# Selective scans: projection by token halves, the other direction added at another turn, part of B's diagonals on ScalarE

## The chip, the cores and the metric

The kernel runs on one core of a Trainium2 chip. The engines used here are TensorE (PE in the profile, with its weight loads as PEld), VectorE (DVE), ScalarE (ACT), GpSimd (POOL) and the queue of SyncE (SP), which issues the DMAs. Each works through its own list of instructions in order, and waits on semaphores for the others. The metric is the device time of one execution in microseconds.

## The reference, cut to what matters

The network has two layers; the change touches the scans in the second one's mixer. For each of K = 4 directions, with D = 256 channels, N = 16 states, R = 8 ranks and L = 4096 tokens in each of B = 4 images:

```python
x_dbl = jnp.einsum('bkdl,kcd->bkcl', xs, x_proj_w)
dts_r, Bs, Cs = (x_dbl[:, :, :R], x_dbl[:, :, R:R + N], x_dbl[:, :, R + N:])
dts = jnp.einsum('bkrl,kdr->bkdl', dts_r, dt_proj_w)
dt = jax.nn.softplus(dts + dt_proj_b[None, :, :, None])
A = -jnp.exp(A_logs).reshape(K, d, N)
def step(h, inp):
    dt_l, u_l, B_l, C_l = inp
    dA = jnp.exp(dt_l[..., None] * A)
    h = h * dA + (dt_l * u_l)[..., None] * B_l[:, :, None, :]
    y = jnp.einsum('bkdn,bkn->bkd', h, C_l)
    return (h, y)
ys = ys + Ds.reshape(1, K, d, 1) * xs
y = ys[:, 0] + ys[:, 2][..., ::-1]
y1 = ys[:, 1] + ys[:, 3][..., ::-1]
```

Directions 2 and 3 run backwards through the tokens, 0 and 1 forwards; 0 and 2 go by rows of the image, 1 and 3 by columns.

## The kernel before, in words

Attention, a recurrent layer, the inputs of the scans, the scans, their outputs and the experts follow one another. All that is told here lies in the function `scans`.

The tokens of the four images, padded to 4125 each, are cut into blocks of 125, and four blocks make a window of W = 500 tokens: 33 windows a direction, 132 in all, in the order of directions 2, 3, 0, 1. A window has 16 tiles: four groups of four states (q), by four blocks. One tile holds, for 128 channels on the partitions, both halves of the channels (h), four states and one block, 1016 elements wide with the places for the carried values.

The order of the work is written out by hand: the loop at the end runs over turns p, and every instruction stands where the turn puts it. In turn p the following are issued, in this order: `finish` of a window whose turn it is; the `fill` of tile p + 1; the `carry` of tile p − 1; the scan of tile p; two sums; `times_c` of tile p; the load of C for tile p + 5; the load of the other direction; the decays; and steps of `project` for the windows ahead. A window's tiles start at its turn 0, and 16 turns later the next one's do. So turns are counted modulo 16 here: a step that `project` yields as −14 is in turn 2 of the window before its own.

What a tile needs:

- `fill` (line 1291): TensorE makes dt·u·B for the tile. The weights are dt·u turned so that tokens are on the partitions (`dtu_t`), the moving operand is a diagonal matrix of B's values (`b_diag`, and `b_other` with the halves of the partitions exchanged), 32 x 128 at a time. Between them TensorE adds zeros to y (line 1300).
- decays (line 1256): ScalarE's exponentials, into a ring of 12 tiles, three or two in each of most turns; none in turns 2, 3, 10 and 11.
- scan (line 1315): one VectorE instruction over the tile.
- `carry` (line 1336): ScalarE copies the last state of tile p − 1 into the ring of decays, for the next tile of the same states. That tile is two turns on, so the carry has one scan's time to be done without a wait.
- `times_c` (line 1349): GpSimd multiplies the states by C, which DMAs have spread over the partitions (`c_ring`, from `c_rows` in device memory).
- sums (line 1366): TensorE adds the products into y, in even turns, 16 records at a time. The last sum of a window is in turn 8 of the next.

What a window needs is in `project`, a generator whose steps are spread over 40 turns: load u; x_ps = w_x·u (line 1144, one 500-column product per half of the channels, turns 15 and 1); copy it to `xd` on ScalarE (line 1149, turn 2), with a row of ones; send C's rows to device memory (line 1151); copy B's rows in pieces of 32 tokens (`b_rows`, line 1158, turn 3); the dt projection (line 1163, turn 9); softplus by exponentials and logarithms on ScalarE (lines 1182 to 1190, turns 10 to 12) and a maximum on VectorE, which writes dt (line 1195, turns 13 and 14); dt·u on GpSimd (line 1198, turn 15); turn B's rows (line 1203, turn 1); make `b_diag` (turns 2 and 3); copy dt·u in pieces (`quarters`, line 1227); exchange halves by two DMAs (line 1232, turn 4); turn dt·u (line 1239, turn 5) and copy it (line 1241, turn 6). x_ps, the dt projections, B's turned rows and dt·u's all use one PSUM tile `mm` of two banks. `b_diag` is made as a product of B's values with an identity of 32 columns, `ident32`: VectorE does two of the four groups of partitions' tokens in turn 2 (line 1213, 1024 elements) and one in turn 3 (512 elements); GpSimd does the fourth from a copy (`b_sb`, line 1206).

At the end of a window, `add_other` (line 1377) adds to y, on TensorE, either D·u (direction 2) or the result of the opposite direction (0 and 1); for direction 3 it returns at once. It stands in turn 23 of the window, turn 7 of the next. What it adds is loaded in turn 13. `finish` (line 1387) copies y to `sum` on ScalarE in turn 25, turn 9 of the next, the first instruction of that turn, and stores it.

Of the kernel before, what the change touches and what calls it, by code (L numbers as in the profile page):

```python
# [19 lines left out]
F32 = mybir.dt.float32  # L20
AF = mybir.ActivationFunctionType
# [5 lines left out]
P = 128  # L27
# [7 lines left out]
D, N, R, K = 256, 16, 8, 4  # L35
ND = D // P
NB, BLOCK = 4, 125
DT_ROWS = 0, 96
LP = -(-L // BLOCK) * BLOCK
E, HID, TOPK = 64, 512, 8  # L40
NHC = HID // P
# [957 lines left out]
def scans(ctx, tc, a, us, ys, flag):  # L999
# [10 lines left out]
    nc = tc.nc  # L1010
    cst = ctx.enter_context(tc.tile_pool(name="sc_c", bufs=1))
# [5 lines left out]
    NW = B * JB // NB  # L1017
    assert NW * NB == B * JB
    TILES = Q * NB
    HALF = P // 2  # L1020
    S = T + 2
    LANE = 4 * S

    RINGS = 12, 4, 12
    C_RING = 8
    SKIP = CH - LANE

    ident = cst.tile([P, P], F32, name="ident")
# [8 lines left out]
        rows = slice(HALF * i, HALF * i + HALF)  # L1037
        nc.vector.tensor_copy(fold[rows], ident[rows, rows])
    w_x = loaded(nc, cst, a["w_x"], "w_x")
    w_dt = cst.tile([P, K, P], F32, name="w_dt")  # L1040

    one = cst.tile([P, 1], F32, name="one")
    nc.vector.reduce_sum(one, ident[:, R : R + 1 + DT_ROWS[1] : DT_ROWS[1]], axis=AX.X)
    for h, row in enumerate(DT_ROWS):
        nc.sync.dma_start(w_dt[row : row + R + 1], a["w_dt"][:, :, h * P : (h + 1) * P])
    ds = loaded(nc, cst, a["ds"], "ds")
    na = loaded(nc, cst, a["a_logs"], "a_logs")
    nc.scalar.activation(na, na, AF.Exp)
# [72 lines left out]
    def quartered(of, to, turned):  # L1121

        for half in range(2) if turned else (None,):
            i = NB if half is None else NB // 2
            yield (
                to if half is None else to[:, :, 2 * half : 2 * half + 2],
                bass.AP(
                    of.tensor,
                    of.offset + (0 if half is None else (2 - 2 * half) * T),
                    [of.ap[0], [STEP, NS], [T, i], [1, 32]],  # L1130
                ),
            )

    def project(v):

        k = v.k
        yield -BEFORE
        v.u = work.tile([P, ND, W], F32, tag="u", name="u")
        for b, of, to in v.pieces:
            nc.sync.dma_start(v.u[:, :, to], us[b][k % 2][:, :, of])  # L1140
        x_ps = mm[:, 0]
        for h, turn in enumerate((-33, -31)):
            yield turn
            nc.tensor.matmul(
                x_ps[:, :W], w_x[:, h, k, :], v.u[:, h, :], start=h == 0, stop=h == ND - 1
            )
        yield -30
        xd = work.tile([P, W], F32, tag="xd", name="xd", bufs=1)
        nc.scalar.activation(xd, x_ps[:, :W], AF.Identity, bias=one)
        v.c_rows = dram.tile([NB, N, T], F32, tag="c", name="c_rows")  # L1150
        nc.sync.dma_start(
            v.c_rows.rearrange("i n t -> n i t"),
            xd[64 : 64 + N].rearrange("n (i t) -> n i t", i=NB),
        )
        yield -29
        b_rows = work.tile([32 + N, NS, NB, 32], F32, tag="b_rows", name="b_rows", bufs=1)
        for to, of in quartered(xd[32 : 32 + N], b_rows[32:], False):
            nc.scalar.copy(to, of)
        yield -23
        pts = mm[:, :, :W]  # L1160
        for h, row in enumerate(DT_ROWS):
            rows = slice(row, row + R + 1)
            nc.tensor.matmul(pts[:, h], w_dt[rows, k, :], xd[rows], start=True, stop=True)
        yield -22
        e = work.tile([P, ND, W], F32, tag="e", name="e", bufs=1)
        if v is todo[0]:

            nc.scalar.preload_act_table_set("natural_log_exp_and_others")
        low = work.tile([P, ND * NS * P], F32, tag="low", name="low", bufs=1)
        bound = low[:, : ND * W].rearrange("p (h t) -> p h t", h=ND)  # L1170
        if flag is None:
            nc.scalar.activation(e, pts, AF.Relu, scale=-1.0, bias=most)
            nc.scalar.activation(e, e, AF.Exp, scale=-1.0, bias=most)
            nc.scalar.activation(bound, e, AF.Copy, scale=-0.5, bias=1.0)
            yield -21
            nc.gpsimd.tensor_mul(bound, bound, e)
            for h in range(ND):
                nc.vector.tensor_max(bound[:, h], pts[:, h], bound[:, h])
            nc.scalar.activation(pts, e, AF.Ln, bias=1.0)
        else:  # L1180
            nth = todo.index(v)
            nc.scalar.activation(
                bound, pts, AF.Exp, scale=-1.0, accum_out=largest[:, 1, nth : nth + 1]
            )
            nc.scalar.activation(e, pts, AF.Exp, accum_out=largest[:, 0, nth : nth + 1])
            yield -21
            nc.scalar.activation(bound, bound, AF.Ln, bias=half)
            nc.scalar.activation(pts, e, AF.Ln, bias=1.0)
            yield -20
            nc.scalar.activation(bound, bound, AF.Exp, scale=-1.0)  # L1190
        yield -19
        v.dt = work.tile([P, ND, W], F32, tag="dt", name="dt")
        for h, turn in enumerate((-19, -18)):
            yield turn
            nc.vector.tensor_max(v.dt[:, h], pts[:, h], bound[:, h])
        yield -17
        dtu = work.tile([P, ND, W], F32, tag="e", name="dtu", bufs=1)
        nc.gpsimd.tensor_mul(dtu, v.dt, v.u)
        yield -15
        b_ps = mm[:, 1, : NS * N].rearrange("p (s n) -> p s n", s=NS)  # L1200
        for i in range(NS):
            part = b_rows[32 : 32 + N, i].rearrange("n i t -> n (i t)")
            nc.tensor.transpose(b_ps[:, i, :], part, ident[32 : 32 + N, 32 : 32 + N])
        yield -14
        b_sb = work.tile([P, N], F32, tag="b_sb", name="b_sb")
        nc.scalar.copy(b_sb, b_ps[:, NS - 1, :])
        v.b_diag = work.tile([P, NS, N, 32], F32, tag="b_diag", name="b_diag")
        quarters = work.tile([P, ND, NS, NB, 32], F32, tag="low", name="quarters", bufs=1)
        for turn, i in ((-14, 0), (-13, 2)):
            yield turn  # L1210
            h = i // 2
            w = 2 - h
            nc.vector.tensor_mul(
                v.b_diag[:, i : i + w].rearrange("p s n t -> p (s n) t"),
                b_ps[:, i : i + w]
                .rearrange("p s (n o) -> p (s n) o", o=1)
                .to_broadcast([P, w * N, 32]),
                ident32.rearrange("p (o t) -> p o t", o=1).to_broadcast([P, w * N, 32]),
            )
            if h:  # L1220
                nc.gpsimd.tensor_mul(
                    v.b_diag[:, NS - 1],
                    b_sb.rearrange("p (n o) -> p n o", o=1).to_broadcast([P, N, 32]),
                    ident32.rearrange("p (o t) -> p o t", o=1).to_broadcast([P, N, 32]),
                )
            for to, of in quartered(dtu[:, h], quarters[:, h], h):
                nc.scalar.copy(to, of)
# [12 lines left out]
        yield -10  # L1240
        nc.scalar.copy(v.dtu, turned)
# [164 lines left out]
    with tc.manual_schedule():  # L1406
# [58 lines left out]
        def sums(p):  # L1465

            g, turn = divmod(p - 10, NB)
            for g, n in ((g, 0), (g, 1)) if turn == 0 else ((g, 2), (g, 3)) if turn == 2 else ():
                if g in range(len(pairs)):
                    sum_of(pairs[g], n)  # L1470
            w, turn = divmod(p - 23, TILES)
            if turn == 0 and w in range(len(todo)):
                add_other(todo[w])

# [317 lines left out]
def laid_out(i):  # L1792
# [15 lines left out]

    def apart(w):

        out = np.zeros((K, P, D), w.dtype)
        out[:, 32 : 32 + N], out[:, 64 : 64 + N] = w[:, R : R + N], w[:, R + N :]
        for row in DT_ROWS:
            out[:, row : row + R] = w[:, :R]
        return out

    def turned(w):
# [23 lines left out]
        "w_x": apart(i["L1_conv_x_proj_w"]).reshape(K, P, ND, P).transpose(3, 2, 0, 1),  # L1841
# [36 lines left out]
```

## Time and profile before

| | us |
|---|---|
| time, median of 3 executions (lowest to highest) | 9429.01 (9418.11 to 9439.51) |
| the profiled execution: time, span | 9417.97, 9416.2 |
| first scan begins, last scan ends | 3582.72, 8748.46 |
| PE, DVE, ACT, POOL busy in the span | 8705.1, 8349.7, 7121.8, 4993.6 |
| in 4900 to 6140 (direction 3): PE, DVE, ACT, POOL | 1181.2, 1224.9, 1068.6, 1192.9 of 1240 |
| in 6180 to 7420 (direction 0): PE, DVE, ACT, POOL | 1184.5, 1205.3, 1047.2, 1165.7 of 1240 |
| one scan, of 2112 | 2.256 |
| one product with C on GpSimd, of 2112 | 2.152 |
| one decay on ScalarE, of 4224 | 0.715 |

In the scans all four engines are nearly always busy, and PE's busy time includes pipelined ends. So sums of busy time decide little there: it is the order inside of a window, the same 132 times, that shows who waits. The groups of instructions give durations, the timeline of each engine gives starts, and a bracket behind a line of the timeline gives the idle time before it and what ended it.

### The profile page before, as it was taken

To read this page: it belongs to the slowest core of one execution; us is meant where nothing else is said; L and a number is where in the kernel's file an instruction comes from. 1 tells how busy PE (TensorE), PEld (TensorE's weight loads), DVE (VectorE), ACT (ScalarE), POOL (GpSimd) and SP (SyncE) were. 2 spreads that over 40 slices of the span, in tenths; PEclk is the share of its full clock that TensorE was granted. 3 is DMA by queue.
4 is the path that set the end of the run, shared out by engine and by line. 5 is a ranking of instruction groups with operands and counts; after the bars stand their busy time and mean duration, and the time that the engine had idled before them with its cause. 6 is when DMAs were issued, how large, how long until landed. Compare 5 with 4: busy or idle time off the path is not lost. (4 is left out here: it accounts for less than half of the span.)

```text
span 9416.2 us, 237919 instructions
## 1 busy us (share of the span) xinstructions
PE 8705.1 (92%) x102194; PEld 4318.3 (46%) x102194; DVE 8349.7 (89%) x5102; ACT 7121.8 (76%) x10926; POOL 4993.6 (53%) x2433
## 2 busy tenths in 40 slices
PE   7999999999988888999999999999999999999766
PEld 3333333333323334555555555555555555555223
DVE  6999999999978318999999999999999999999764
ACT  3888888888856467888888888888888888888321
POOL 0000000000001017999999999999999999999100
PEclk8999999999999898999999999999999999999887
DMA  4000000000011335666666656666666666666634
GB/s 169 36 8 35 8 10 35 8 8 8 10 52 56 115 135 151 173 173 173 172 171 167 165 164 162 161 171 173 173 173 173 173 173 173 173 173 168 231 111 184
DMA packets 530963, 1164.77 MB, mean 124 GB/s; under 512 B 76818, under 2 KB 444506, under 8 KB 502106
## 3 DMA queue, kind: packets, MB, share of 16 engines
q1 hardware_dynamic: 529882, 1149.30, 42.0%
q8 instruction: 807, 13.22, 0.6%
q14 instruction: 274, 2.24, 0.1%
HBM read 828.51 MB, written 182.15 MB: 107 GB/s over the span
## 5 line engine op out<-in xcount | busy, mean ns | idle before, releaser
L1315 DVE TENSOR_TENSOR_SCAN states<-decays,db 128x1016 f32<-128x1016 f32 x2112 | 4671.3, 2256 | 109.1 <-ACT decays L1336 60.5
L1349 POOL TENSOR_TENSOR products<-states,c_ring 128x1000 f32<-128x1000 f32 x2112 | 4459.8, 2152 | 294.8 <-DVE states L1315 173.4
L1256 ACT ACTIVATE decays<-dt,a_logs 128x500 f32<-128x500 f32 x4224 | 3018.2, 715 | 86.6 <-DVE states L1315 0.5
L1291 PEld LDWEIGHTS db<-b_diag,dtu_t 32*128 32x128 f32 x16896 | 2051.1, 187 | 1523.1 <-DVE states L1315 927.4
L1291 PE MATMUL db<-b_diag,dtu_t 32*128 32x128 f32 x16896 | 2429.4, 283 | 245.1 <-DVE states L1315 226.2
L1291 PE MATMUL db<-b_other,dtu_t 32*128 32x128 f32 x16896 | 2454.2, 284 | 0.0
L1300 PE MATMUL y<-zeros 32*128 32x128 f32 x14720 | 2122.0, 283 | 0.0
L1291 PEld LDWEIGHTS db<-b_other,dtu_t 32*128 32x128 f32 x16896 | 2048.0, 186 | 0.3 <-issue 0.2
L1366 PE MATMUL y<-products,ident 64*64 64x500 f32 x16896 | 2018.8, 592 | 1.1 <-POOL products L1349 1.1
L1300 PEld LDWEIGHTS y<-zeros 32*128 32x128 f32 x14720 | 1771.9, 186 | 0.0
L342 DVE TENSOR_TENSOR total<-total,ring 128x2048 f32<-128x2048 f32 x768 | 1706.9, 2285 | 32.3 <-ACT ring L304 31.6
masks.py:197 POOL MEMSET ident<- 128x128 f32 x6 | 1.2, 206 | 2915.6 <-SPq L181 2622.9
L304 ACT ACTIVATE ring<-sa 128x2048 f32<-128x2048 f32 (+3 forms) x667 | 1153.7, 1738 | 273.8 <-PE sa L289 262.2
L314 PE MATMUL av<-ring,v_at 128*32 128x256 f32 (+1 forms) x16128 | 1096.1, 389 | 6.2 <-ACT o L323 5.7
L1366 PEld LDWEIGHTS y<-products,ident 64*64 64x64 f32 x16896 | 541.2, 132 | 696.7 <-issue 568.1
L314 PEld LDWEIGHTS av<-ring,v_at 128*32 128x32 f32 x16128 | 421.4, 109 | 950.9 <-issue 748.9
L304 ACT ACTIVATE ring<-sb 128x1536 f32<-128x1536 f32 (+2 forms) x585 | 800.6, 1375 | 73.6 <-PE sb L289 63.8
L289 PE MATMUL sa<-q_at,k_at 32*128 32x512 f32 x4898 | 701.4, 640 | 20.6 <-issue 14.3
L289 PE MATMUL sb<-q_at,k_at 32*128 32x512 f32 x3294 | 624.0, 641 | 0.0
L1336 ACT COPY decays<-states 128x8 f32<-128x8 f32 x2048 | 405.3, 198 | 212.2 <-DVE states L1315 196.0
L289 PEld LDWEIGHTS sa<-q_at,k_at 32*128 32x128 f32 x4898 | 192.4, 183 | 354.6 <-issue 177.1
L339 DVE TENSOR_TENSOR total<-ring 128x2048 f32<-128x2048 f32 x128 | 288.6, 2287 | 67.0 <-ACT ring L304 66.6
(217 smaller groups left out, 8023.7 us busy)
## 6 DMA issues: line engine op xcount, KB each, us to landing
c_ring<-c_rows SPq DMA_DIRECT2D x2112, 250.0 KB, 4.8
b_other<-b_diag SPq DMA_DIRECT2D x264, 512.0 KB, 6.2
weights<-in_w SPq DMA_DIRECT2D x32, 1024.0 KB, 13.0
u<-u_r SPq DMA_DIRECT2D x60, 500.0 KB, 6.4
y_r<-sum SPq DMA_DIRECT2D x60, 500.0 KB, 4.7
u<-u_c SPq DMA_DIRECT2D x60, 500.0 KB, 6.4
y_c<-sum SPq DMA_DIRECT2D x60, 500.0 KB, 5.1
x<-x SPq DMA_DIRECT2D x96, 256.0 KB, 2.6
```

What stands on the lines that cost most here:

```text
L289: nc.tensor.matmul(s[:, m, :], k[rows, tokens(t)], q[rows, chunk(chunk_state["c"])], start=True, stop=True,)
L304: nc.scalar.activation(ring[:, lo : lo + n, :], s[:, at : at + n, :], AF.Exp)
L314: nc.tensor.matmul(chunk_state["av"][rows, some], chunk_state["v"][:, t, rows], ring[:, at + i, some], start=t == 0, stop=t == NJ - 1 and ...
L339: nc.vector.tensor_add(total, sums[g - 2], w)
L342: nc.vector.tensor_add(sums[g % 2], sums[g % 2], w)
L1256: nc.scalar.activation(to, dt, AF.Exp, scale=scale)
L1291: nc.tensor.matmul(bank.rearrange("p (n t) -> p n t", n=4)[:, :, to : to + 32], v.dtu[rows, h, s, :], b[rows, s, 4 * self.q : 4 * self.q + ...
L1300: nc.tensor.matmul(y[:, idle // 2, :P], zeros[rows], zeros[rows], start=False, stop=False)
L1315: nc.vector.tensor_tensor_scan(order(self.slot(states)), order(self.slot(decays, shift)), order(self.db[:, SKIP + shift :][:, : 2 * LANE]) ...
L1336: nc.scalar.copy(self.edge(later.slot(decays), later.v.into), last)
L1349: nc.gpsimd.tensor_mul(to, h, c)
L1366: nc.tensor.matmul(to, ident[rows, rows], of, start=begins, stop=ends)
```

## The change

Four edits in `scans`, and a matching layout of two weights:

1. The projection works by halves of the tokens. The rows of a direction (dt's 8 and the one of ones, B's 16, C's 16) fill 64 rows in place of 128. Tokens 0 to 249 of a window go to the lower 64 partitions, tokens 250 to 499 to the upper 64, so `xd` is 250 wide. All of x_ps is made in turn 15; `xd` and C's rows follow in turn 1, `b_rows` (two copies) in turn 2. The dt projection reads partitions 0 and 64, and a bank of `mm` holds both halves of the channels for one half of the tokens; `in_halves` gives the views for it.
2. `add_other` stands in turn 19 in place of 23.
3. Of the 32 columns of B's diagonals, VectorE and GpSimd make 24 (FEW).
4. ScalarE makes the other eight, four behind VectorE's product in turn 2 and four behind that in turn 3, each an ACTIVATE of B's 64 turned values times one column of `ident32`.

```diff
-DT_ROWS = 0, 96
+DT_ROWS = 0, 64
...
-    HALF = P // 2
+    HALF, WH = P // 2, W // 2
...
+    FEW = 24
...
-    w_dt = cst.tile([P, K, P], F32, name="w_dt")
+    w_dt = cst.tile([P, K, ND, P], F32, name="w_dt")
...
+    def in_halves(of):
+        return of.rearrange("p h (j t) -> p h j t", j=2)
...
-        x_ps = mm[:, 0]
-        for h, turn in enumerate((-33, -31)):
-            yield turn
-            nc.tensor.matmul(
-                x_ps[:, :W], w_x[:, h, k, :], v.u[:, h, :], start=h == 0, stop=h == ND - 1
+        yield -33
+        x_ps = mm[:, 0, :WH]
+        for h in range(ND):
+            for j in range(2):
+                nc.tensor.matmul(
+                    x_ps[HALF * j : HALF * j + HALF],
+                    w_x[:, h, k, :],
+                    v.u[:, h, j * WH : (j + 1) * WH],
+                    start=h == 0,
+                    stop=h == ND - 1,
+                )
+        yield -31
+        xd = work.tile([P, WH], F32, tag="xd", name="xd", bufs=1)
+        nc.scalar.activation(xd, x_ps, AF.Identity, bias=one)
+        v.c_rows = dram.tile([NB, N, T], F32, tag="c", name="c_rows")
+        for j in range(2):
+            nc.sync.dma_start(
+                v.c_rows[2 * j : 2 * j + 2].rearrange("i n t -> n i t"),
+                xd[HALF * j + 48 : HALF * j + 48 + N].rearrange("n (i t) -> n i t", t=T),
             )
         yield -30
-        xd = work.tile([P, W], F32, tag="xd", name="xd", bufs=1)
-        nc.scalar.activation(xd, x_ps[:, :W], AF.Identity, bias=one)
...
-        yield -29
         b_rows = work.tile([32 + N, NS, NB, 32], F32, tag="b_rows", name="b_rows", bufs=1)
-        for to, of in quartered(xd[32 : 32 + N], b_rows[32:], False):
-            nc.scalar.copy(to, of)
+        for j in range(2):
+            of = xd[HALF * j + 32 : HALF * j + 32 + N]
+            nc.scalar.copy(
+                b_rows[32:, :, 2 * j : 2 * j + 2],
+                bass.AP(of.tensor, of.offset, [of.ap[0], [STEP, NS], [T, 2], [1, 32]]),
+            )
         yield -23
-        pts = mm[:, :, :W]
-        for h, row in enumerate(DT_ROWS):
-            rows = slice(row, row + R + 1)
-            nc.tensor.matmul(pts[:, h], w_dt[rows, k, :], xd[rows], start=True, stop=True)
+        pts = mm[:, :, :W].rearrange("p j (h t) -> p h j t", h=ND)
+        for h in range(ND):
+            for j, row in enumerate(DT_ROWS):
+                rows = slice(row, row + R + 1)
+                nc.tensor.matmul(pts[:, h, j], w_dt[rows, k, h, :], xd[rows], start=True, stop=True)
...
             nc.vector.tensor_mul(
-                v.b_diag[:, i : i + w].rearrange("p s n t -> p (s n) t"),
+                v.b_diag[:, i : i + w, :, :FEW].rearrange("p s n t -> p (s n) t"),
                 b_ps[:, i : i + w]
                 .rearrange("p s (n o) -> p (s n) o", o=1)
-                .to_broadcast([P, w * N, 32]),
-                ident32.rearrange("p (o t) -> p o t", o=1).to_broadcast([P, w * N, 32]),
+                .to_broadcast([P, w * N, FEW]),
+                ident32[:, :FEW]
+                .rearrange("p (o t) -> p o t", o=1)
+                .to_broadcast([P, w * N, FEW]),
             )
             if h:
                 nc.gpsimd.tensor_mul(
-                    v.b_diag[:, NS - 1],
...
+                    v.b_diag[:, NS - 1, :, :FEW],
...
+            for t in range(FEW + 4 * h, FEW + 4 * h + 4):
+                nc.scalar.activation(
+                    v.b_diag[:, :, :, t].rearrange("p s n -> p (s n)"),
+                    b_ps.rearrange("p s n -> p (s n)"),
+                    AF.Identity,
+                    scale=ident32[:, t : t + 1],
                 )
...
-            w, turn = divmod(p - 23, TILES)
+            w, turn = divmod(p - 19, TILES)
             if turn == 0 and w in range(len(todo)):
                 add_other(todo[w])
```

More of the change, by code (lines that the diff above doesn't have):

```diff
@@ L1039, in scans @@
     w_x = loaded(nc, cst, a["w_x"], "w_x")
-    w_dt = cst.tile([P, K, P], F32, name="w_dt")
+    w_dt = cst.tile([P, K, ND, P], F32, name="w_dt")
     one = cst.tile([P, 1], F32, name="one")
     nc.vector.reduce_sum(one, ident[:, R : R + 1 + DT_ROWS[1] : DT_ROWS[1]], axis=AX.X)
-    for h, row in enumerate(DT_ROWS):
-        nc.sync.dma_start(w_dt[row : row + R + 1], a["w_dt"][:, :, h * P : (h + 1) * P])
+    for row in DT_ROWS:
+        nc.sync.dma_start(
+            w_dt[row : row + R + 1], a["w_dt"].rearrange("r k (h d) -> r k h d", h=ND)
+        )
     ds = loaded(nc, cst, a["ds"], "ds")
@@ L1146, in project @@
+        yield -31
[3 more added lines that the diff above has]
+        for j in range(2):
+            nc.sync.dma_start(
+                v.c_rows[2 * j : 2 * j + 2].rearrange("i n t -> n i t"),
+                xd[HALF * j + 48 : HALF * j + 48 + N].rearrange("n (i t) -> n i t", t=T),
             )
         yield -30
-        xd = work.tile([P, W], F32, tag="xd", name="xd", bufs=1)
@@ L1149, in project @@
[L1149 to L1154, printed above, removed]
-        yield -29
-        b_rows = work.tile([32 + N, NS, NB, 32], F32, tag="b_rows", name="b_rows", bufs=1)
-        for to, of in quartered(xd[32 : 32 + N], b_rows[32:], False):
-            nc.scalar.copy(to, of)
@@ L1159, in project @@
-        yield -23
-        pts = mm[:, :, :W]
-        for h, row in enumerate(DT_ROWS):
-            rows = slice(row, row + R + 1)
-            nc.tensor.matmul(pts[:, h], w_dt[rows, k, :], xd[rows], start=True, stop=True)
+        b_rows = work.tile([32 + N, NS, NB, 32], F32, tag="b_rows", name="b_rows", bufs=1)
+        for j in range(2):
[3 more added lines that the diff above has]
+                bass.AP(of.tensor, of.offset, [of.ap[0], [STEP, NS], [T, 2], [1, 32]]),
+            )
@@ L1169, in project @@
         low = work.tile([P, ND * NS * P], F32, tag="low", name="low", bufs=1)
-        bound = low[:, : ND * W].rearrange("p (h t) -> p h t", h=ND)
+        bound = in_halves(low[:, : ND * W].rearrange("p (h t) -> p h t", h=ND))
+        e = in_halves(e)
         if flag is None:
@@ L1192, in project @@
         v.dt = work.tile([P, ND, W], F32, tag="dt", name="dt")
+        dt = in_halves(v.dt)
         for h, turn in enumerate((-19, -18)):
             yield turn
-            nc.vector.tensor_max(v.dt[:, h], pts[:, h], bound[:, h])
+            nc.vector.tensor_max(dt[:, h], pts[:, h], bound[:, h])
         yield -17
@@ L1221, in project @@
                 nc.gpsimd.tensor_mul(
-                    v.b_diag[:, NS - 1],
-                    b_sb.rearrange("p (n o) -> p n o", o=1).to_broadcast([P, N, 32]),
-                    ident32.rearrange("p (o t) -> p o t", o=1).to_broadcast([P, N, 32]),
+                    v.b_diag[:, NS - 1, :, :FEW],
+                    b_sb.rearrange("p (n o) -> p n o", o=1).to_broadcast([P, N, FEW]),
+                    ident32[:, :FEW].rearrange("p (o t) -> p o t", o=1).to_broadcast([P, N, FEW]),
+                )
+            for t in range(FEW + 4 * h, FEW + 4 * h + 4):
[4 more added lines that the diff above has]
+                    scale=ident32[:, t : t + 1],
                 )
@@ L1809, in apart @@
     def apart(w):
[L1811 to L1814, printed above, removed]
+        out = np.zeros((K, P // 2, D), w.dtype)
+        out[:, :R] = w[:, :R]
+        out[:, 32 : 32 + N], out[:, 48 : 48 + N] = w[:, R : R + N], w[:, R + N :]
         return out
@@ L1840, in laid_out @@
         "b_conv": i["L1_conv_conv_b"].reshape(ND, P).T,
-        "w_x": apart(i["L1_conv_x_proj_w"]).reshape(K, P, ND, P).transpose(3, 2, 0, 1),
+        "w_x": apart(i["L1_conv_x_proj_w"]).reshape(K, P // 2, ND, P).transpose(3, 2, 0, 1),
         "w_dt": np.concatenate(
```

## The prediction

> **What bounds the kernel now.** I read the engines' shares first, then the slices of the span, then the scans' instructions in order of time, engine by engine. The scans (line 1315) run from 3582.72 to about 8748 us, 5166 of 9416.2 us, and the change touches nothing else. In the stretch 4900 to 6140 us (direction 3) VectorE is busy 1224.94 of 1240 us, in 6180 to 7420 us (direction 0) 1205.27. The hidden share is small, so the order of a single window decides. A window has 16 scans. Here is VectorE in one of direction 0 and in one of direction 3; a gap in brackets is idle time and what ended it:
>
> ```profile
> 7009.98 0.68 DVE L1195 TENSOR_TENSOR dt<-mm,low 128x500 f32<-128x500 f32 x1 [0.22 <-ACT low L1190]
> ...
> 7022.14 1.22 DVE L1213 TENSOR_TENSOR b_diag<-mm,ident 128x1024 f32<-128x1024 f32 x1
> 7023.28 2.26 DVE L1315 TENSOR_TENSOR_SCAN states<-decays,db 128x1016 f32<-128x1016 f32 x1
> 7025.45 0.67 DVE L1213 TENSOR_TENSOR b_diag<-mm,ident 128x512 f32<-128x512 f32 x1
> 7026.04 13.28 DVE L1315 TENSOR_TENSOR_SCAN states<-decays,db 128x1016 f32<-128x1016 f32 x6
> 7039.94 4.47 DVE L1315 TENSOR_TENSOR_SCAN states<-decays,db 128x1016 f32<-128x1016 f32 x2 [0.62 <-ACT decays L1336]
> ```
>
> ```profile
> 5453.42 0.68 DVE L1195 TENSOR_TENSOR dt<-mm,low 128x500 f32<-128x500 f32 x1 [0.23 <-ACT low L1190]
> ...
> 5465.59 1.22 DVE L1213 TENSOR_TENSOR b_diag<-mm,ident 128x1024 f32<-128x1024 f32 x1
> ...
> 5491.85 0.68 DVE L1195 TENSOR_TENSOR dt<-mm,low 128x500 f32<-128x500 f32 x1 [0.22 <-ACT low L1190]
> ```
>
> Dt to dt is 38.43 us in direction 3. In direction 0 the scan after the 0.62 us gap comes 39.26 us after its like (7000.68). Direction 3 is the one for which `add_other` returns at once. So both stalls end with ScalarE, and ScalarE in the same windows says why:
>
> ```profile
> 7021.00 0.17 ACT L1206 COPY b_sb<-mm 128x16 f32<-128x16 f32 x1 [0.73 <-PE mm L1144]
> 7021.07 0.64 ACT L1227 COPY quarters<-dtu 128x512 f32<-128x512 f32 x1
> 7023.40 0.68 ACT L1149 ACTIVATE xd<-mm,one 128x500 f32<-128x500 f32 x1 [1.69 <-DVE b_diag L1213]
> 7024.07 0.73 ACT L1227 COPY quarters<-dtu 128x256 f32<-128x256 f32 x2
> ...
> 7038.75 0.99 ACT L1387 COPY sum<-y 128x1000 f32<-128x1000 f32 x1 [1.62 <-PE y L1366]
> 7039.64 0.21 ACT L1336 COPY decays<-states 128x8 f32<-128x8 f32 x1
> ```
>
> ```profile
> 5475.51 0.99 ACT L1241 COPY dtu_t<-mm 128x1024 f32<-128x1024 f32 x1
> 5476.40 0.20 ACT L1336 COPY decays<-states 128x8 f32<-128x8 f32 x1
> ...
> 5481.36 0.99 ACT L1387 COPY sum<-y 128x1000 f32<-128x1000 f32 x1 [0.78 <-PE y L1366]
> ```
>
> The copy of y waits for TensorE; behind it stands the carry (L1336) that the next scan but one needs. From that carry to dt ScalarE has no gap: 7000.38 to 9.98 is 9.60 us (5482.25 to 5491.85 too). So a window is a loop: dt to the first b_diag product 12.16 us, product to the copy of y (call it A), 0.89 from copy to carry, 9.60 to dt. A is 16.61 in direction 0 (7022.14 to 7038.75) and 15.77 in direction 3; the loop gives 39.26 and 38.43, as seen. **A is what the change must shorten.** TensorE just before the copy, with the moved work:
>
> ```profile
> 7034.68 1.07 PE L1377 MATMUL y<-other,ident 64*64 64x500 f32 x8
> 7036.77 1.91 PE L1366 MATMUL y<-products,ident 64*64 64x500 f32 x16
> ```
>
> **The change part by part** (times from the start of the first b_diag product).
>
> *VectorE's columns.* The products take 1.224 us for 1024 elements and 0.665 for 512 (direction-3 means 1.225 and 0.666), a line of 1.09 ns per element. For 768 and 384 it gives 0.944 and 0.525: 0.28 + 0.14 = 0.42 us less per window. GpSimd's product, 1.07 us for 512 elements, loses about 0.27 and is covered: its queue has 1.35 us of gaps per window.
>
> *ScalarE's columns.* Eight instructions of 128x64. No row shows one. PSUM to SBUF 1000 elements take 0.991, a copy of 512 0.635, so 64 about 0.21; xd with an operand per partition takes 0.677 for 500, about 0.10 over that line, so 0.31. Independent copies start 0.10 before the last one ends (the two quarters: 0.41 each, 0.73 together), so I take 0.21 each. Below stands the carry's 0.10; above the decays, which do not overlap: three take 2.21, 0.75 apart for 500 elements, so 0.39 for 64. The copies' form is the nearest, hence 0.21. The xd row also shows an ordering: xd only reads mm, as the product does, and yet starts 0.04 after the product ends. I take it that the columns are ordered likewise: four behind the first product, then the second product, then four more.
>
> [...]
>
> *Projection by halves.* xd becomes 250 elements, about 0.21 shorter, and moves one turn up, in front of the product that held it. There it puts off a carry and b_sb by 0.37; b_sb then ends some 1.4 us before the product wants it. b_rows (0.63) becomes two copies, by the 128x256 row 0.31 apart, so 0.62. TensorE's four 500-column pieces in line 1144 (two of 1.10 us together per turn) become eight of 250 on two halves of the array. That column halves run side by side the sum's 64*64 shapes show: 16 records of 0.59 in 1.91. So 1.10 us goes out of turn 1. The dt matmuls keep their length. SP issues one DMA more (0.32 us), but c_rows leaves 3.5 us sooner: SP stood from 7018.14 to 7024.10 with c_ring loads behind it. Those, needed five turns later, and c_rows itself, needed a window later, are covered.
>
> *Other side added at turn 19.* Its 1.07 us go from turn 7 to turn 3. There, in direction 3, TensorE idles 0.60 waiting for a scan, and 1.10 from turn 1 stand beside it: room for 1.07. Behind it in TensorE's queue is the fill of the scan after next, which that 1.70 covers; without it that scan would start about 0.5 late. The loads stay at turn 13; at 7006.31 to 7009.41 SP issues them, they land 5.6 us later at most, so 9 us before 7024. The last sum then ends where direction 3's does (15.71) less 0.42: 15.29.
>
> *Sum for A by ScalarE.* 0.98 first product and wait; four columns 0.84 (1.82); quarters 0.54 (2.36); b_rows 0.62 (2.98); carry 0.10 (3.08); then it waits for the second product, which ends at 3.32 − 0.28 + 0.53 = 3.57, so 3.61; four columns (4.45); quarters 0.62 (5.07); twice a carry with three decays 2.22 (9.51); carry, two decays and dtu_t, 5474.01 to 5476.40, 2.39 (11.90); carry and two decays 1.48 (13.38); carry and three decays 2.22: **A = 15.60**. TensorE's 15.29 is earlier, so ScalarE sets A, alike in all directions. Of the gap before the second four, 0.53 hides any extra cost of the first four.
>
> Loop: 15.60 + 0.89 + 9.60 + 12.16 = 38.25. Of 132 windows 99 have the other side: 99 x (16.61 − 15.60) = 100, 33 x 0.17 = 6. Together −106 us: 9417.97 (the profiled execution; span 9416.2) becomes 9312. That execution stood 11 us under the median 9429, so for a median I forecast 9323.
>
> **The rivals.** *VectorE becomes the bound again.* If nothing holds the columns behind the products, ScalarE starts them in its 1.69 us wait. Direction 3 then runs at 38.43 less 0.42 less part of its idle (15 us in 32 windows, 0.47): about 37.75. 99 x 1.51 + 33 x 0.68 = 172 off, 9257. Against it: the xd wait.
>
> *The columns are dear.* At 0.21 + d each, A = 15.60 + 4d + max(0, 4d − 0.53). At 0.39 A is 16.51: 99 x 0.10 gained, 33 x 0.74 lost, 14 us slower, 9443 at worst; it decides at d = 0.165 (0.375 each), where nothing is gained. Between 0.30 and 0.39, 9370 to 9443. For it, the decays' rows; against, the copies'.
>
> [...]
>
> *The columns wait for GpSimd (slower).* Decays, interleaved in one ring, wait for each other though no element is shared. If the second four are ordered so behind GpSimd's share of the same tile, they start when that ends. It ran at 7028.37 for 1.09, gapless queue ahead, so new at about 7.1 against 3.61: A rises 3.5 to 19.1. 99 x 2.5 + 33 x 3.3 = 357 slower: 9786. It decides from 0.8 us of wait on. Against: the quarters, interleaved too, do not wait.
>
> *The halves run one after the other.* 2.2 us in turn 15, with 0.54 idle behind and about 0.2 more before a scan: 0.36 per window late. 99 x 0.65 − 33 x 0.19 = 58 off: 9371.
>
> **How the numbers follow.** Forecast 0.62, its own range by 0.17 to 0.26 per column 9302 to 9350. VectorE-bound 0.08 (9257). Dear 0.12, of which about 0.07 is still faster, 0.04 the same and 0.01 slower. GpSimd 0.10. Halves in line 0.08. From no change this kernel can be told at about 0.2%, 19 us. Faster 0.62 + 0.08 + 0.08 + 0.07 = 0.85, same 0.04, slower 0.11. The range 9255 to 9395 takes in all but GpSimd and half of dear, 0.16.
>
> **What would show it.** The gap of 0.62 before the scan gone or near 0.2, in every direction one window length near 38.25; before dt a wait for low of about 0.6, not 0.22; sum not waiting for y; columns 0.31 long, the first after a gap of some 2.4 us for b_diag. Wrong if ScalarE waits for GpSimd between the columns, if columns stand 0.38 apart, or if y still ends after 16.5.

## The result, and the profile after

The changed kernel takes 9320.45 us, the median of four executions (9305.85 to 9322.77). The kernel before, run beside it, takes 9432.17 (9418.11 to 9439.51). The ratio is 0.988, with a 95% interval of 0.9863 to 0.9897. The forecast was 9323, within 9255 to 9395, and faster.

The profiled execution of the changed kernel took 9321.16 us (span 9319.2), 96.8 less than that of before. From first scan to last the time falls from 5165.7 to 5053.9, which is 112 less; the first scan starts 15.9 later (3598.60 against 3582.72). That part was not changed: in the other kernels below, which leave it alone too, the first scan starts anywhere from 3583.3 to 3603.4.

All of it comes from the length of a window. Here are VectorE, ScalarE and two lines of TensorE, from the timeline of the changed kernel, for one window of direction 0. The columns are start, duration, engine and line, operation and tiles; a bracket holds the idle time ahead and what ended it.

```profile
6997.24 0.68 DVE L1214 TENSOR_TENSOR dt<-mm,low 128x500 f32<-128x500 f32 x1 [0.45 <-ACT low L1208]
...
7009.33 0.93 DVE L1232 TENSOR_TENSOR b_diag<-mm,ident 128x768 f32<-128x768 f32 x1
7010.18 2.26 DVE L1343 TENSOR_TENSOR_SCAN states<-decays,db 128x1016 f32<-128x1016 f32 x1
7012.35 0.53 DVE L1232 TENSOR_TENSOR b_diag<-mm,ident 128x384 f32<-128x384 f32 x1
7012.89 13.33 DVE L1343 TENSOR_TENSOR_SCAN states<-decays,db 128x1016 f32<-128x1016 f32 x6
```

```profile
6986.78 0.97 ACT L1415 COPY sum<-y 128x1000 f32<-128x1000 f32 x1
6987.65 0.21 ACT L1364 COPY decays<-states 128x8 f32<-128x8 f32 x1
...
7007.35 0.45 ACT L1160 ACTIVATE xd<-mm,one 128x250 f32<-128x250 f32 x1
...
7007.79 0.17 ACT L1225 COPY b_sb<-mm 128x16 f32<-128x16 f32 x1
7010.30 0.99 ACT L1248 ACTIVATE b_diag<-mm,ident 128x64 f32<-128x64 f32 x4 [2.33 <-DVE b_diag L1232]
7011.10 0.65 ACT L1255 COPY quarters<-dtu 128x512 f32<-128x512 f32 x1
7011.76 0.83 ACT L1171 COPY b_rows<-xd 16x256 f32<-16x256 f32 x2
7012.60 0.21 ACT L1364 COPY decays<-states 128x8 f32<-128x8 f32 x1
7012.92 0.99 ACT L1248 ACTIVATE b_diag<-mm,ident 128x64 f32<-128x64 f32 x4
7013.72 0.74 ACT L1255 COPY quarters<-dtu 128x256 f32<-128x256 f32 x2
...
7024.93 0.97 ACT L1415 COPY sum<-y 128x1000 f32<-128x1000 f32 x1
```

```profile
6984.65 1.91 PE L1394 MATMUL y<-products,ident 64*64 64x500 f32 x16
...
7001.25 1.06 PE L1151 MATMUL mm<-u,w_x 128*64 128x250 f32 x8
```

Three things are to be seen. The scan that began after a gap of 0.62 us now stands in a run of six without a gap. The copy of y (L1415) has no wait before it: the last sum of y ends at 6986.56, and the copy starts 0.22 later, when ScalarE is free. And the wait has moved to dt, whose 0.22 us for `low` have become 0.45. Copy to copy is 38.15 us, against 39.26.

The groups by shape, from 3700 to 8600 us, give the prices (count, busy time, mean ns of one, idle time before them):

```profile
L1248 ACT ACTIVATE b_diag<-mm,ident 128x64 f32<-128x64 f32 x1024 | 253.6, 375 | 315.5 <-DVE b_diag L1232 301.0
L1232 DVE TENSOR_TENSOR b_diag<-mm,ident 128x768 f32<-128x768 f32 x128 | 119.2, 931 | 0.0
L1232 DVE TENSOR_TENSOR b_diag<-mm,ident 128x384 f32<-128x384 f32 x128 | 68.0, 531 | 0.0
L1171 ACT COPY b_rows<-xd 16x256 f32<-16x256 f32 x254 | 103.9, 409 | 3.0
L1242 POOL TENSOR_TENSOR b_diag<-b_sb,ident 128x384 f32<-128x384 f32 x128 | 109.6, 856 | 0.0
```

The terms of the loop, as medians over the windows:

| us | before, other side to add | before, direction 3 | forecast | after, every direction |
|---|---|---|---|---|
| first product to copy of y (A) | 16.61 | 15.77 | 15.60 | 15.60 |
| copy to carry | 0.89 | 0.89 | 0.89 | 0.87 |
| carry to dt | 9.60 | 9.60 | 9.60 | 9.60 |
| dt to first product | 12.16 | 12.16 | 12.16 | 12.08 |
| loop | 39.26 | 38.43 | 38.25 | 38.14 |

### The profile page after: what moved, and what is told of

It is laid out like the page before. It is cut to its first block, busy times and chain, and to the rows that moved or that the text cites. A ratio compares the mean times of both kernels' runs of the same rounds, so it can differ in the third digit from the quotient of the medians.

```text
span 9319.2 us, 241459 instructions
## 1 busy us (share of the span) xinstructions
PE 8594.7 (92%) x103250; PEld 4327.6 (46%) x103250; DVE 8279.5 (89%) x5102; ACT 7300.2 (78%) x12114; POOL 4960.2 (53%) x2433
## 3 DMA queue, kind: packets, MB, share of 16 engines
q14 instruction: 285, 2.33, 0.1%
## 5 line engine op out<-in xcount | busy, mean ns | idle before, releaser
L1248 ACT ACTIVATE b_diag<-mm,ident 128x64 f32<-128x64 f32 x1056 | 261.5, 375 | 322.9 <-DVE b_diag L1232 308.2
```

What stands on the lines that cost most here:

```text
L1248: nc.scalar.activation(v.b_diag[:, :, :, t].rearrange("p s n -> p (s n)"), b_ps.rearrange("p s n -> p (s n)"), AF.Identity, scale=ident32[ ...
```

## The experiments

Theory: a window is a loop that ScalarE closes. What ends A last (the sum of y on TensorE, or ScalarE's own list between the first product and the copy of y) sets the window, and VectorE has slack. Rivals: VectorE's shorter products are what was gained; and TensorE's shorter turn 1 is what was gained, by whichever engine is freed.

The comparisons are with the kernel before, on the same chip. The ratio and the medians need not agree to the last 0.1%. Loops are those of the profiled execution.

| kernel | median us | beside before | ratio (95%) | loop, direction 0 / 3 |
|---|---|---|---|---|
| the change | 9320.45 | 9432.17 | 0.988 (0.9863 to 0.9897) | 38.14 / 38.14 |
| e1: other side sooner alone | 9367.57 | 9428.78 | 0.9944 (0.9928 to 0.9961) | 38.42 / 38.43 |
| e2: halves alone | 9573.45 | 9428.78 | 1.0155 (1.0138 to 1.0172) | 40.80 / 38.33 |
| e3: change without columns | 9347.63 | 9428.78 | 0.9919 (0.9903 to 0.9936) | 38.31 / 38.31 |
| e4: change, other side late | 9402.03 | 9428.78 | 0.9969 (0.9957 to 0.9982) | 38.90 / 38.17 |
| e5: columns from a copy | 9286.76 | 9431.71 | 0.9846 (0.983 to 0.9863) | 37.91 / 37.91 |
| e6: e5, copy of y a turn later | 9256.33 | 9431.71 | 0.9818 (0.9802 to 0.9834) | 37.65 / 37.65 |
| e7: each column twice | 9501.08 | 9431.71 | 1.0072 (1.0055 to 1.0088) | 39.57 / 39.57 |
| e8: halves and filler | 9418.76 | 9431.71 | 0.9986 (0.9976 to 0.9996) | 39.16 / 38.31 |
| e9: e6 with twelve columns | 9280.55 | 9430.55 | 0.9844 (0.9827 to 0.986) | 37.72 / 37.72 |
| e10: halves, small filler | 9414.58 | 9430.55 | 0.9982 (0.9973 to 0.9992) | 39.16 / 38.31 |

### e1: the other side sooner, and nothing else

The kernel before, with one number changed:

```diff
-            w, turn = divmod(p - 23, TILES)
+            w, turn = divmod(p - 19, TILES)
             if turn == 0 and w in range(len(todo)):
                 add_other(todo[w])
```

> The kernel before with the other side added in turn 19 alone. Theory (a window is a loop, and the copy of y sets it): TensorE has the 0.6 us gap of turn 3 for it but not the 1.10 of turn 1, so the fill of turn 4 starts about 0.4 late and the last sum ends near 15.9 after the first product's start instead of 16.54: A about 15.97 and not 15.77, loop 38.6 in the three directions that have the other side, 38.43 in direction 3; about 63 us less than the 9432 of before. Rival (the gains come from busy time taken off VectorE, the place of the addition is worth little without it): within 15 us of before. Rival (the move needs the halves): no gain or a loss, because the fill behind the addition makes scans late.

It takes 61 us off, over half of the change's 112. A falls to 15.77 in every direction, the value that direction 3 had, where I had expected 15.97. Here is e1's timeline for one window of direction 0, VectorE's first product, then ScalarE's copy of y:

```profile
6877.75 1.23 DVE L1213 TENSOR_TENSOR b_diag<-mm,ident 128x1024 f32<-128x1024 f32 x1
```

```profile
6893.52 0.99 ACT L1387 COPY sum<-y 128x1000 f32<-128x1000 f32 x1 [0.78 <-PE y L1366]
```

From 6877.75 to 6893.52 is 15.77, and y is still what the copy waits for. VectorE's products are as long as before (1.23), so this part of the gain owes nothing to them. The loops alone would give 99 x (39.26 − 38.42) = 83 us; 14 windows of 39.9, in each of which the trace shows a stretch of TensorE at half clock, take back 14 x 1.5 = 21. So e1 should give 62, and 61 was measured.

### e2: the halves, and nothing else

The changed kernel, without ScalarE's columns and with the other side back in its old turn:

```diff
-    FEW = 24
+    FEW = 32
...
-            for t in range(FEW + 4 * h, FEW + 4 * h + 4):
-                nc.scalar.activation(
...
-            w, turn = divmod(p - 19, TILES)
+            w, turn = divmod(p - 23, TILES)
```

> The projection by halves alone: no columns on ScalarE, the other side in turn 23. Theory: the 1.10 us that leave turn 1 are given back at once, since the fill of turn 4 waits for the scan of turn 3 in any case; y's last sum ends where it ended, A stays 16.61 and 15.77, within 10 us of before. Rival (TensorE's busy time counts, it is 95% busy here): 1.1 us per window or a good part of it, 70 to 145 us less.

I expected next to nothing and got 145 us more. It is no instruction that grew: the clock that TensorE was granted fell, to 0.50 for 3.41 us at a time. Its timeline, TensorE in two stretches of one window of direction 0, then ScalarE's copy of y and VectorE's scan behind:

```profile
6793.43 1.91 PE L1387 MATMUL y<-products,ident 64*64 64x500 f32 x16
...
6797.87 0.37 PE L1312 MATMUL db<-b_diag,dtu_t 32*128 32x128 f32 x1 [1.44 <-DVE states L1336]
...
6799.19 3.32 PE L1387 MATMUL y<-products,ident 64*64 64x500 f32 x16
```

```profile
6803.74 4.43 DVE L1336 TENSOR_TENSOR_SCAN states<-decays,db 128x1016 f32<-128x1016 f32 x2 [1.01 <-ACT decays L1277]
```

```profile
6812.66 0.99 ACT L1408 COPY sum<-y 128x1000 f32<-128x1000 f32 x1 [2.13 <-PE y L1387]
```

The same 16 records of the sum take 1.91 us before the gap of 1.44 and 3.32 after it. The table of stretches shows the clock in the column behind the five engines' busy times (PE, PEld, DVE, ACT, POOL, each with its count); then come the DMA share and GB/s:

```profile
6795.25:6798.66 3.41, 1.97 (x49) 1.77 (x48) 3.41 (x4) 0.95 (x3) 3.41 (x2) 1.00 0.51 187
6798.67:6802.08 3.41, 3.41 (x28) 1.09 (x22) 3.41 (x2) 2.88 (x5) 3.41 (x4) 0.50 0.12 40
...
6836.21:6839.62 3.41, 1.62 (x39) 1.43 (x42) 3.41 (x4) 0.95 (x4) 3.41 (x3) 1.00 0.65 205
6839.63:6843.04 3.41, 3.41 (x27) 1.46 (x28) 3.41 (x2) 2.87 (x6) 3.41 (x3) 0.50 0.05 16
```

After a stretch of 3.41 us in which TensorE was busy for 1.6 to 2.0 comes one of 3.41 us at half clock. The half-clock stretches begin at 6757.71, 6798.67 and 6839.63, 40.96 us apart, which is 12 x 3.413. The window has become 40.80 us, so the gap meets nearly the same place in the grid of stretches each time, and all but a few of the windows of direction 0 are hit (31 such stretches in its 33 windows). In direction 3, where the window is 38.33, the phase drifts, and 12 of 33 windows are hit (39.6). From 3600 to 8700 us 97 stretches, 331 us, pass at half clock.

The step in the kernel is plain. The 1.10 us that left turn 1 open up TensorE's idle time in turn 3, where the fill waits for a scan: 0.60 us became 1.44. In the changed kernel `add_other` sits in that very gap.

### e3 and e4: the change without its columns, and without its move

```diff
-    FEW = 24
+    FEW = 32
```

> The kernel after without ScalarE's columns (all 32 by VectorE and GpSimd): halves and the addition in turn 19. Theory: the addition fits, every direction runs like direction 3 before: A 15.77, loop 38.43, 83 us less than before; the columns are worth the other 30 to 38. Rival (VectorE's 0.42 us per window are the gain): only half of the 112, so about 9375.

```diff
-            w, turn = divmod(p - 19, TILES)
+            w, turn = divmod(p - 23, TILES)
```

> The kernel after with the other side added in turn 23 again. Theory: y is late again in the three directions that have it, less the 0.38 by which VectorE is sooner: A about 16.2, loop 38.8 there, 38.14 in direction 3; about 60 us over the kernel after, near 9382. Rival (columns and halves carry the gain): within 20 us of the kernel after, 9320.

Without columns 81 of the 112 us stay, with A at 15.74; 12 windows of direction 3, where no other side fills the gap, are at 39.6 and cost 12 x 1.3 = 16 us. So the columns are worth some 30 us: the loop gives 132 x 0.17 = 22, and the changed kernel has one such window in place of 12, 11 x 1.3 = 14, together a little more than was measured. With the other side late 27 of the 112 stay: A is 16.32 in direction 0 and 15.61 in direction 3, and ScalarE waits for y again. I had expected about 9382 and got 9402: y, not ScalarE, ends A there, so of what the products save only 0.29 us reaches the window, and five windows of 40.5, each with a stretch at half clock, cost another 5 x 1.6 = 8 us. Most of the gain hangs on the move.

### e5 and e6: take the columns out of their wait

The columns wait 2.33 us for VectorE's product, though they only read B's turned values as it does. In e5 all of those values are copied once, in place of the quarter that GpSimd uses, and the columns read the copy:

```diff
-        b_sb = work.tile([P, N], F32, tag="b_sb", name="b_sb")
-        nc.scalar.copy(b_sb, b_ps[:, NS - 1, :])
+        b_all = work.tile([P, NS, N], F32, tag="b_sb", name="b_sb")
+        nc.scalar.copy(b_all, b_ps)
+        b_sb = b_all[:, NS - 1, :]
...
-                    b_ps.rearrange("p s n -> p (s n)"),
+                    b_all.rearrange("p s n -> p (s n)"),
```

> The kernel after, but b_sb copies all 64 of B's turned values to SBUF and the columns read that copy instead of mm. Theory (two readers of mm are ordered one behind the other): nothing holds the columns any more, the 2.34 us in which ScalarE waits for the first product are used, and ScalarE reaches the copy of y some 2 us sooner; then y's last sum, 15.29 us behind the scan, sets A: 15.44, loop 37.98 in place of 38.14, about 20 us under the kernel after. Rival (the columns were held by something else, the tile that they write): they start no sooner, loop 38.14. Rival (ScalarE was the only bound): loop 37.6, 70 us less.

e6 adds to it a copy of y one turn later:

```diff
-            w, turn = divmod(p - 25, TILES)
+            w, turn = divmod(p - 26, TILES)
             if turn == 0 and w in range(len(todo)):
                 finish(todo[w])
```

> The one before, and y copied in turn 26 instead of 25, behind the decays of turn 9. Theory: the copy no longer waits for y's last sum, so neither of the two waits is left on ScalarE; VectorE's own time sets the loop, 38.14 less its 0.45 before dt and its 0.18 before scans, 37.5 to 37.7: 60 to 80 us under the kernel after, near 9250. Rival: the next window's first sum, in the same turn, waits for the copy on TensorE, the fills behind it are late, and no more is gained than without it, about 9300.

ScalarE in a window of e5:

```profile
6833.21 0.21 ACT L1225 COPY b_sb<-mm 128x64 f32<-128x64 f32 x1
...
6833.90 1.12 ACT L1249 ACTIVATE b_diag<-b_sb,ident 128x64 f32<-128x64 f32 x4 [0.48 <-PE db L1320]
...
6836.48 1.12 ACT L1249 ACTIVATE b_diag<-b_sb,ident 128x64 f32<-128x64 f32 x4
...
6850.10 0.99 ACT L1416 COPY sum<-y 128x1000 f32<-128x1000 f32 x1 [0.78 <-DMA c_ring<-c_rows]
```

VectorE's first product begins at 6834.76 in this window, so the first four columns start before it, and the 2.33 us are gone. A is 15.34, and now the copy of y waits once more: the bracket names a DMA, but the last sum of y ended 0.07 us before the copy began, as in the kernel before. So with ScalarE relieved TensorE's sum ends A, at about the 15.29 that the prediction had for it. In e6 the copy stands a turn later, nothing waits for y, and this is VectorE:

```profile
6836.82 0.65 DVE L1214 TENSOR_TENSOR dt<-mm,low 128x500 f32<-128x500 f32 x1
```

```profile
L1344 DVE TENSOR_TENSOR_SCAN states<-decays,db 128x1016 f32<-128x1016 f32 x2063 | 4547.9, 2253 | 42.2 <-ACT decays L1365 29.8 <-PE db L1320 7.2 <-POOL products L1378 0.6
```

No wait before dt is left, and from 3700 to 8560 us VectorE is busy 4817.71 of 4860. Both steps go the way that the loop theory asks: −34 and −64 us against the changed kernel's median, where I had expected some 20 for the first and 60 to 80 for both. At 9256.33 e6 beats both kernels.

### e7: twice the work on ScalarE

```diff
-            for t in range(FEW + 4 * h, FEW + 4 * h + 4):
+            for t in 2 * list(range(FEW + 4 * h, FEW + 4 * h + 4)):
```

> The kernel after with each of ScalarE's eight columns made twice. Theory (ScalarE sets the loop): 0.20 us for each, the first four hidden only by the 0.12 that ScalarE waits before the second four: 0.8 + 0.68 = 1.48 us per window, loop 39.6, 195 us over the kernel after, 9515. By the prediction's formula, in which 0.53 is hidden, 1.07 us and 9460. Rival (VectorE or TensorE is the bound, ScalarE has 10% to spare): within 20 us of the kernel after.

Every column is made twice, with the same values. ScalarE and VectorE in one window:

```profile
6977.22 1.82 ACT L1248 ACTIVATE b_diag<-mm,ident 128x64 f32<-128x64 f32 x8 [2.33 <-DVE b_diag L1232]
...
6980.45 1.81 ACT L1248 ACTIVATE b_diag<-mm,ident 128x64 f32<-128x64 f32 x8
...
6993.26 0.97 ACT L1415 COPY sum<-y 128x1000 f32<-128x1000 f32 x1
```

```profile
6980.64 13.40 DVE L1343 TENSOR_TENSOR_SCAN states<-decays,db 128x1016 f32<-128x1016 f32 x6 [0.83 <-POOL products L1377]
```

The first product starts at 6976.25, so A is 17.01 here. It grew by 1.42 us for 2 x 0.83 of added columns, and the window by 1.43: what ScalarE has between the product and the copy of y passes almost whole into the loop, and the copy still does not wait for y. If the shorter products on VectorE carried the gain, work on ScalarE would have been hidden.

### e8 and e10: fill the gap of e2

To e2 a few matmuls of zeros are added, where the change puts the other side. They add nothing to y:

```diff
+            w, turn = divmod(p - 19, TILES)
+            if turn == 0 and w in range(len(todo)):
+                for _ in range(4):
+                    nc.tensor.matmul(
+                        todo[w].y[:, 0, :P], zeros, zeros, start=False, stop=False
+                    )
```

> The halves alone, with four products of zeros (128 columns each, added to y) on TensorE in turn 3, so about 1 us more work in the 1.44 us gap that the halves leave there. Theory: the halves alone were slower only because TensorE's granted clock falls to half for 3.4 us after that gap, once per window; the filler closes the gap, the loop is 39.2 where the other side is added and 38.3 in direction 3: within 15 us of before, 150 us under the halves alone. Rival (the halves' own products or their order cost 1.5 us per window): stays near 9570.

e10 has one in place of four (`range(1)`):

> The halves with one product of zeros in turn 3 in place of four, so that about 1.2 us of the 1.44 us gap stay open. Theory (the clock falls when a gap takes too large a part of one 3.4 us stretch): in the kernel after, direction 3 has a gap of 1.17 us there and lost the clock in one window of 33; so it falls rarely, few windows are longer than 39.2 and 38.3, within 40 us of before. Rival (any gap over about 1 us costs the clock): most windows at 40.8 again, near 9570.

Over 1000 us of direction 0 the table of stretches reads, for e2 and then for e8:

```profile
6400.00:7400.00 1000.00, 913.88 (x13096) 538.95 (x13092) 935.16 (x492) 818.36 (x1573) 907.34 (x442) 0.96 0.60 168
```

```profile
6400.00:7400.00 1000.00, 938.81 (x13796) 572.39 (x13798) 967.99 (x511) 844.04 (x1634) 942.54 (x460) 1.00 0.64 175
```

With more work on TensorE the kernel is 155 us shorter than e2, no stretch from 3700 to 8600 us is at half clock, and the window is 39.16. The one matmul of e10 does as well. It leaves a gap of 1.01 us, not the 1.2 that I had expected, and the one half-clock stretch in the same time, at 6169, stands behind a gap of 1.67 at the change from direction 3 to 0. So the cost of e2 was the clock, and the halves alone, with the gap closed or cut to 1.01, are worth 13 to 16 us.

### e9: more columns

e6 with `FEW = 20`, and six columns behind each product on ScalarE in place of four:

```diff
-    FEW = 24
+    FEW = 20
...
-            for t in range(FEW + 4 * h, FEW + 4 * h + 4):
+            for t in range(FEW + 6 * h, FEW + 6 * h + 6):
```

> The kernel with the columns from the copy and the later copy of y, with twelve columns on ScalarE in place of eight. Theory (VectorE sets the loop there, 37.65): its two products lose about 0.13 and 0.07 us more, ScalarE's 0.8 more fits into its waits: loop 37.45 to 37.5, some 20 to 25 us less, near 9233. Rival (ScalarE or TensorE's fills are the bound already): no gain or a loss.

I expected a further gain, and got 9280.55 where e6 has 9256.33 (ratios 0.9844 and 0.9818). The scans' group, from 3700 to 8560 us:

```profile
L1344 DVE TENSOR_TENSOR_SCAN states<-decays,db 128x1016 f32<-128x1016 f32 x2050 | 4519.2, 2253 | 95.3 <-PE db L1320 41.6 <-ACT low L1205 26.2 <-ACT decays L1285 25.8
```

VectorE's products are shorter (798 and 465 ns), but the scans now wait 95.3 us in place of 42.2, for TensorE's fills and for ScalarE. Thirteen windows are at 39.4 with a stretch at half clock, 1.7 longer than the others, which is 22 us. The others are at 37.72, 0.07 above e6, though they were expected some 0.2 below it; what holds them, these runs do not settle.

## Why the prediction was right, and where it was not

**The loop** was right: A is 15.60 in all directions, as summed, and what was a wait for y has become a chain on ScalarE. e1, e4, e5 and e7 move it in the way that the theory asks. The rival that VectorE's products carry the gain falls with e1 and e7 as an account of the whole; the columns' share of some 30 us does come from scans that end sooner, so that y does (in e4, where y ends A, it fell by 0.29).

**The sum for A** holds because its errors met a cover. Against the starts in the window shown above (first product at 7009.33):

| from the first product, us | forecast | measured |
|---|---|---|
| first columns start | 0.98 | 0.97 |
| `quarters` | 1.82 | 1.77 |
| `b_rows` | 2.36 | 2.43 |
| carry | 2.98 | 3.27 |
| second four columns | 3.61 | 3.59 |
| `quarters` | 4.45 | 4.39 |
| copy of y | 15.60 | 15.60 |

A column was 375 ns long where 0.31 was forecast, but four took 0.99 and stand 0.205 apart, as the row of independent copies had suggested; that was the price that mattered. `b_rows` was mis-sized: the two copies do not overlap (409 ns each, 0.83 together) where 0.62 was forecast. The first `quarters` took 0.65, not 0.54, and the carry 0.21, not 0.10. Together they used up most of the cover before the second four columns, which came to 0.12 us and not 0.53. Here that cost nothing, since the second product ended the wait; in e7, where the cover mattered, the growth was 1.42 and not the 1.07 that the old cover would give.

**Columns held behind the product**: right. The wait for b_diag was 2.33 us against "some 2.4". e5, where the columns read SBUF, starts them 0.86 us ahead of the product (6833.90 against 6834.76), so the wait was an order between readers of `mm`. The 1.69 us of `xd`, from which the prediction took it, was a wait for a reader of the other half of `mm` (`xd` reads `mm[:, 0]`, the product `mm[:, 1]`), while the columns read the half that the product reads. What makes the order, and how much of `mm` it takes in, the runs do not show. The VectorE-bound rival described what a release of the columns would bring: about 9257. e6 reached 9256, but it took a later copy of y as well; release alone (e5) gave 9287.

**GpSimd, halves one after the other, dear columns**: none came. The second four columns wait for VectorE alone. The halves ran side by side: eight records in 1.06 us. GpSimd's product fell to 856 ns, 0.22 less for 0.27.

**TensorE's 1.10 us out of turn 1** was the step that needed more than I gave it. I counted it as room for the other side, and as no gain of its own. That holds in the change, but alone it cost 145 us (e2), for the gap of 1.44 us that it leaves in turn 3 and the 3.41 us at a clock of 0.50 behind it. In the change the move fills that gap, and the columns shorten it: in e4, which has them and not the move, it is 1.17 us, 0.27 less, about what VectorE's first product lost, and the clock was lost in five of 99 windows. Where I costed an edit at nothing I asked what covers it, but not what idle time on TensorE does to its clock.

**The gain and its size.** The loop fell by 1.12 in 99 windows and by 0.29 in 33, which is 120 us; the forecast had 106. The rest of that is dt to product, 12.08 for 12.16, and copy to carry, 0.87 for 0.89, 132 x 0.10 = 13. Of the 120, by the loops of the runs, the move gives 99 x 0.84 = 83 (e1), the halves 14 (e8: 39.26 to 39.16, 38.43 to 38.31) and the columns 132 x 0.17 = 22 (e3). The measured 112 are less than 120, since the ends of the scans gained nothing: the first two windows take 71.0 us from first product to third, against 67.1, the last one 44.1 against 42.7, and one window (39.32) met a half-clock stretch. Of the signs to look for, the gap of 0.62 went altogether (I had said "gone or near 0.2"), the window is 38.14 for 38.25, and the wait before dt rose to 0.45, for "about 0.6". That the median came within 3 us of 9323 is partly luck. The 13 us that the sum left out and the some 7 that the ends of the scans and the slow window took back nearly cancel, and the part ahead of the scans moves by 20 us from run to run: the profiled execution was forecast at 9312 and took 9321.16, with a first scan 15.9 later.

## What to carry to other kernels

In a loop that is written out over engines, look for the one chain that closes it, and cost an edit by what it does to that chain; then ask what ends it next. Here the sum of y, ScalarE's list and VectorE itself took turns within 0.8 us of one window (38.43 in e1, 38.14, 37.91 in e5, 37.65 in e6), and small edits (the columns behind the move, a copy that frees them, a later copy of y) each moved the bound on. Work taken from an engine can be a loss if its idle time comes to lie in one piece: the halves alone cost 145 us that way, and gained 13 to 16 once a few products of zeros stood in the gap. So look for where the idle time goes, and whether other work can be moved there.

## What the runs showed of the hardware that was not expected

In e2 a gap of 1.44 us, once a window, was followed, in 31 of the 33 windows of direction 0, by 3.41 us in which TensorE's clock was half (0.50 in the table, the sum 3.32 us in place of 1.91); TensorE was mostly busy for 1.6 to 2.0 us of the stretch of 3.41 ahead. A gap of 1.17 us (direction 3 of the changed kernel) did it in one window of 33, and the gap of 1.01 in e10 in none.

Nor did the clock fall only behind a gap. In e1 the 14 windows of 39.9 lose the clock behind a stretch in which the profile shows TensorE busy without a break, 18.8 to 19.1 us after the first product. Here are three stretches of one of them:

```profile
6504.13:6507.54 3.41, 3.41 (x63) 1.96 (x57) 2.97 (x3) 2.38 (x5) 3.41 (x2) 1.00 0.97 257
6507.54:6510.95 3.41, 3.41 (x44) 2.35 (x44) 3.41 (x2) 3.23 (x7) 3.25 (x2) 1.00 0.94 312
6510.96:6514.37 3.41, 3.41 (x25) 1.18 (x20) 2.76 (x2) 3.41 (x7) 3.41 (x3) 0.50 0.96 229
```

The 13 windows of 39.4 in e9 are alike, with TensorE busy for 3.1 to 3.2 us of the stretch ahead. All 27 stretches ahead hold 30 to 32 records of the fills and none of the products of zeros that otherwise stand between them: 44 matmuls in the second line, 63 in the first. So in these 27 windows TensorE lost its clock (0.50) behind a stretch in which the table shows it busy for 3.1 us or more of 3.41. What the clock goes by, no run here shows.

And the loop of e2 kept in step with the slow stretches. Its 97 half-clock stretches lie on a grid of 3.41 us to within 0.01, and its slowed window (40.80) is near to twelve of them (40.96), so that the gap met nearly the same place of the grid each time. In direction 3 neither the loop of 38.3 nor the slowed window of 39.6 is near a multiple (11 are 37.5, 12 are 41.0), and the clock was lost in about one window of three.
